# A two-layer graph network on one core: node degrees from a second load of the adjacency, leftover filter coefficients in 32x32 tiles, and a norm placed later

## The chip, the cores and the metric

One core of a Trainium2 chip, everything in float32. The metric is device microseconds of one execution of the whole program; lower is better. The median of several runs is compared.

## What is computed

The input x holds 128 samples of 128 nodes with 256 features, adj one 128x128 matrix per sample. Two layers follow each other, each as a residual under a layer norm.

```python
# layer 0
in_degrees = jnp.sum(adj, axis=-1)
norm = jnp.power(in_degrees + 1e-06, -0.5)[..., None]
f_hom = jnp.einsum('bnd,de->bne', x, theta) * norm
f_hom = jnp.einsum('bnm,bmd->bnd', adj, f_hom) * norm
f_het = jnp.einsum('bnd,de->bne', x, W_h)
gate = jax.nn.sigmoid(jnp.einsum('bnd,de->bne', x, W_t) + b_t)
out = jax.nn.elu(gate * f_hom + (1.0 - gate) * f_het)
x = _layernorm(x + out)
# layer 1
xc = jnp.transpose(x, (0, 2, 1))
h = relu(bn(conv1d(xc, conv1_w)))              # kernel size 1
h = bn(conv1d(h, conv2_w, pad=8))              # 17 taps along the nodes
x_conv = jnp.transpose(relu(h + xc), (0, 2, 1))
# ... a second branch x_nmp: exp(-distance) of 3 coordinates times relu(x @ w_msg.T)
# ... a GRU cell of [x_conv, x_nmp] and x, then x = _layernorm(x + cell)
```

## The kernel before, in words

Samples go in pairs: pair p holds samples 2p and 2p+1, so there are 64 pairs. Nodes lie on the 128 partitions. The kernel runs in three stages.

**Layer-0 rounds** (`a_round`, from line 597). One round per pair, software-pipelined: round t projects pair t (`l0_project`: products f_ps at L371, gate_ps at L376), mixes it over the adjacency (`l0_mix`, mix_ps L397), finishes pair t-1 (`l0_gate`, `l0_elu`, `l0_norm`), turns and runs conv1 for pair t-3 (`l1_turn`, `l1_front`) and makes the transform of pair t-4 (`l1_analyse`, coef_ps L486). The order on all engines is the order in which the program is written (`tc.manual_schedule` over TensorE, SyncE, DVE, ScalarE and GpSimd), so an instruction that waits holds back what stands behind it on its engine. Eight PSUM banks are handed out in turn.

The degrees of a pair come from its own adjacency tile, which is loaded already transposed: `l0_degrees` transposes the two 128x128 blocks on TensorE (adj_ps, L351), sums them on DVE (L353) and raises the sums to -1/2 on GpSimd (`inv_sqrt`, L206 and L207). It stands at the end of a round for the next pair, and ScalarE multiplies the projection by the result as it evicts f_ps (hom, L380).

The 17-tap convolution along the nodes is done by a transform of length 136 = 128 + 8: `l1_analyse` makes 136 coefficients of every channel and sample from h, ScalarE writes them to the resident tile H (L490), which is laid out as (channel half, coefficient, sample).

The same transform of the filter taps is made inside these rounds, spread over them as extra work. `w_unit` (32 units, about every second round) makes the first 128 coefficients of 4 x 1 filter rows from a tap tile wt: four products of 17 rows by 128 columns in four row tiles of TensorE, 512 columns wide (w_ps, L502), evicted by ScalarE and stored to w_d. The last 8 coefficients, the leftovers, are made by `v_unit` in 19 sets of 7 filter rows: a block table TL of 7 copies of the small transform (built by 14 small DMAs of `leftover_table`) times a second load of the taps (vt, `v_load`), one product of 128x128 by 512 columns (wl_ps, L529), evicted by DVE (L533) and stored by `v_store`.

`l0_norm` of pair t-1 (DVE nb L327, two ScalarE activations L329) follows directly behind the projection of pair t.

**Tap stage** (loop at line 819). For each of 68 pairs of coefficients k, the taps w_d[k] are loaded and multiplied with H: the samples are the columns of the stationary operand. y_ps (L826) takes four products of 256 columns with `coefs(m, c)` as weights. For all but the first k there is a three-product complex form: GpSimd adds the two tap blocks (ws, L834), DVE adds two rows of H (hs, L836), z_ps (L839) multiplies them. In the trace a float32 matmul is two instructions, each with its own weight load.

**Layer-1 groups** (loop from line 1220): the way back of the transform, the second branch and the GRU cell for groups of four samples. The change leaves it alone.

All loads of the rounds and of the tap stage stand in SyncE's queue (SP) in program order; `in_blocks` (L140) loads x in blocks for DVE's 32x32 transpose `l0_turn` of the next pair; every second round `load_blocks` fetches two pairs into the one buffer xb. `w_load` (L170) fills the two buffers of wt.

Of the kernel before, what the change touches and what calls it, by code (L numbers as in the profile page):

```python
# [34 lines left out]
def gnn_layers_kernel(ctx: ExitStack, tc: tile.TileContext, a: dict, out: bass.AP):  # L35
# [49 lines left out]
    A, T = AT2[:, 0, :], AT2[:, 1, :]  # L85
    S = const.tile([P, P], F32, tag="S", name="S")
    SL = const.tile([P, P], F32, tag="SL", name="SL")
    FS = P // TAPS
    TL = taps.tile([P, P], F32, tag="TL", name="TL")
# [5 lines left out]
    vt = taps.tile([P, 2, D], F32, tag="vt", name="vt")  # L95
    wt = [taps.tile([P, 2, D], F32, tag=f"wt{i}", name=f"wt{i}") for i in range(NW)]


# [28 lines left out]
    def bank(name):  # L127
        return ps.tile([P, 512], F32, tag="ps", name=name)
# [75 lines left out]
    def inv_sqrt(dst, src, eps, width):  # L204

        nc.gpsimd.tensor_scalar(dst, src, eps, 1.0, ALU.add, ALU.mult)  # L206
        nc.gpsimd.tensor_tensor(dst, dst, neg_half[:, 0:width], ALU.pow)  # L207
# [79 lines left out]

    def way_back():

        nc.gpsimd.memset(TL, 0.0)  # L290

        nc.gpsimd.memset(vt[96:], 0.0)
# [15 lines left out]
    def leftover_table(i):  # L308

        cols = TL[:, 0 : ML * FS].rearrange("p (r i k) -> p r i k", r=2, i=FS)  # L310
        for r in range(2):
            nc.sync.dma_start(cols[i * TAPS : (i + 1) * TAPS, r, i, :], T[0:TAPS, P + r : M : 2])

    def norm_stats(src, n, name):

# [31 lines left out]
    def l0_degrees(p):  # L347
        s = st[p]
        adj = bank(f"adj_ps_{p}")
        for j in range(J):  # L350
            nc.tensor.transpose(adj[:, nodes(j)], s["adjT"][:, j, :], ident)  # L351
# [4 lines left out]
        inv_sqrt(norm, norm, DEG_EPS, J)  # L356


    def l0_project(p, between, beside):
# [121 lines left out]
    def l1_analyse(p):  # L481
        h = st[p]["h"]
        for j in range(J):
            pa = bank(f"coef_ps_{p}_{j}")
            for c in range(NC):
                nc.tensor.matmul(  # L486
                    pa[:, c * M : (c + 1) * M], lhsT=h[:, j, c * P : (c + 1) * P], rhs=A,
                    start=True, stop=True,
                )
            nc.scalar.activation(  # L490
                H[:, :, :, p * J + j], pa[:, 0 : NC * M].rearrange("p (c m) -> p c m", c=NC), AF.Copy
            )


# [15 lines left out]
        )  # L510


    NV = -(-P // FS)
    s_v = {}

    def v_set(v):

        return FS * v, min(FS, P - FS * v)

    def v_load(v):  # L520
        f, n = v_set(v)
        nc.sync.dma_start(
            vt[0 : n * TAPS],
            a["conv2_wT"].rearrange("(c f) t o -> (f t) c o", c=NC)[f * TAPS : (f + n) * TAPS],
        )

    def v_unit(v):
        pl = bank(f"wl_ps_{v}")
        nc.tensor.matmul(  # L529
            pl, lhsT=TL, rhs=vt.rearrange("p i (o c) -> p i c o", c=NC), start=True, stop=True  # L530
        )
        ol = s_v[v] = taps.tile([ML * FS, NC * D], F32, tag="wl", name=f"wl_o_{v}")
        nc.vector.tensor_copy(ol, pl[0 : ML * FS])  # L533

    def v_store(v):
        ol = s_v.pop(v)
        f, n = v_set(v)
        h = ML // 2
        for r in range(2):
            nc.sync.dma_start(  # L540
                w_d[P // 2 : M // 2, r, f : f + n].rearrange("k f c o -> f k (c o)"),
                ol[r * h * FS : r * h * FS + n * h],
            )


    m_in = []

# [35 lines left out]
    warm = bank("warm_ps")  # L583
    for _ in range(WARM):
        nc.tensor.matmul(warm[:, 0:P], lhsT=ones, rhs=ones, start=True, stop=True)
    units = {2 + 2 * u - 2 * u // NU: u for u in range(NU)}
    rest = [t for t in range(4 + FS, NP - 1) if t not in units]
    units_v = {rest[v * (len(rest) - 1) // (NV - 1)]: v for v in range(NV)}
    hstack = ExitStack()
    H = None  # L590
    E = mybir.EngineType

    SOON = 3
    norms, ways = batch_norms(), way_back()
    tables = table(AT2, (node, lag))

    def a_round(t):
        nonlocal H
        def on(q, work):
            if 0 <= q < NP:  # L600
                work(q)

        def between():
            on(t - 1, l0_gate)
            on(t - 3, l1_turn)
            on(t - 4, l1_analyse)

        def beside():
            if 0 <= t <= SOON:
                l0_turn(t + 1)  # L610
            on(t - 1, l0_elu)
            if 0 <= t < SOON:
                l0_degrees(t + 1)

        if t > 1 and t % 2 == 1 and t + 1 < NP:
            load_blocks(t + 1, 2)
        l0_project(t, between, beside) if t >= 0 else between()
        on(t - 1, l0_norm)
        if t == 0:
            load_blocks(2, 2)  # L620
        if t == -1:
            next(tables)
        if not 0 <= t <= SOON:
            on(t + 1, l0_turn)
        on(t - 3, l1_front)
        on(t - 2, x1_store)
        if t > 0:
            load_x(t)
        if t + 2 < NP:
            if 2 <= t + 2:  # L630
                load(t + 2)
            if 3 <= t < 3 + FS:
                leftover_table(t - 3)
            if t == FS:
                v_load(0)
# [5 lines left out]
        if t - 1 in units_v:  # L641
            v_store(units_v[t - 1])
            if units_v[t - 1] + 1 < NV:
                v_load(units_v[t - 1] + 1)
        if t + 2 < NP:
            on(t - 2, load_back)
        on(t - 3, x1T_store)
        if not 0 <= t < SOON:
            on(t + 1, l0_degrees)
        if t == -1:  # L650
            next(tables, None)
        if t == 0:
            nc.sync.dma_start(conv1_w[:, :, 0:D], a["conv1_wT"].rearrange("(p c) e -> p c e", c=NC))
            nc.sync.dma_start(conv1_w[:, :, D:], a["w_seT"].rearrange("(p c) e -> p c e", c=NC))
            next(norms)
        if t == 1:
            next(norms)
            next(ways)
        if t == NP // 2:
            nc.scalar.dma_start(w_msg, a["w_msgT"].rearrange("(p c) e -> p c e", c=NC))  # L660
            nc.scalar.dma_start(b_msg, a["L1_gnn_b_msg"].partition_broadcast(P))
        on(t, l0_mix)
        if t == 2:
            next(norms, None)
        if t in (4, 5):
            next(ways, None)
        if t == SOON:
            sctx.close()
            hpool = hstack.enter_context(tc.tile_pool(name="hpool", bufs=1))
            H = hpool.tile([P, NC, M, NB], F32, tag="H", name="H")  # L670
        if 0 <= t < 2:
            w_load(t)
        if t - 1 in units and units[t - 1] + NW < NU:
            w_load(units[t - 1] + NW)
        if t in units_v:
            v_unit(units_v[t])
        if t in units:
            if t + 1 < NP:
                w_unit(units[t])

    with tc.manual_schedule(engines={E.PE, E.SP, E.DVE, E.Activation, E.Pool}):
        for t in range(-1, NP):
            a_round(t)
        last = NP - 1
        l1_turn(last - 2)
        w_unit(units[last])
        l0_gate(last)
        l1_analyse(last - 3)
        l1_front(last - 2)
# [3 lines left out]
        l0_elu(last)  # L693
        early = [m_project(0, "gate")]
        m_load(2)
        w_store(units[last])
        m_load(3)
        early[0][0]()
        l0_norm(last)
# [31 lines left out]
    pb = cpool("psB", 6, bctx, space=PSUM)  # L731

    def coefs(m, c):
        return H[:, c, m, :]

    left = cw.tile([P, NB, KD], F32, tag="left", name="left")
    right = cw.tile([P, NB, KD], F32, tag="right", name="right")
# [80 lines left out]
    with tc.manual_schedule(engines={E.Activation, E.Pool}):  # L818
        for k in range(M // 2):
# [12 lines left out]
            else:  # L832
                ws = yb.tile([P, NC, D], F32, tag="ws", bufs=2, name=f"ws_{k}")
                nc.gpsimd.tensor_tensor(ws, w[:, 0], w[:, 1], ALU.add)  # L834
                hs = yb.tile([P, NC, NB], F32, tag="hs", bufs=2, name=f"hs_{k}")
                nc.vector.tensor_tensor(hs, H[:, :, 2 * k, :], H[:, :, 2 * k + 1, :], ALU.add)  # L836
                pz = pb.tile([P, 2, D], F32, tag="py", name=f"z_ps_{k}")
                for c in range(NC):
                    nc.tensor.matmul(  # L839
# [461 lines left out]
```

## Time and profile before

| what | value |
|---|---|
| time, median of 3 runs | 1948.97 us (1948.71 to 1949.96) |
| the profiled execution | 1949.05 us, span 1947.3 us |
| TensorE matmul busy | 1932.2 us (99%) |
| DVE busy | 1497.8 us (77%) |
| ScalarE busy | 744.5 us (38%) |
| GpSimd busy | 674.3 us (35%) |
| granted TensorE clock | 0.998 |
| DMA | 279.64 MB, mean 144 GB/s |

The span is the stretch from the first to the last instruction; the execution's time holds a little more around it. In the lines shown, PE is TensorE's matmul, PEld its weight load (which overlaps PE), ACT is ScalarE, POOL GpSimd, SP SyncE; a "q" behind a name is its sequencer, which issues DMAs. L826 is line 826 of the kernel. A group's line gives engine, operation, out<-in, partitions x elements, count, busy us, mean ns of one, and idle time before it. A timeline's line gives start and length in us of like instructions merged into one. A source's line gives the duration as min/median/max in ns, and the first and last start. Ends of matmuls are modelled and overlap the next one; starts are measured.

### The profile page before, as it was taken

The numbers are of one execution on the slowest core, as the hardware profiler recorded it, in microseconds if no ns is written. First come the engines' busy times: TensorE is split into PE (matmuls) and PEld (weight loads), VectorE is DVE, ScalarE is ACT, GpSimd is POOL, SyncE is SP. The second block draws the span as 40 slices with busy tenths as digits, with TensorE's granted clock in tenths as the row PEclk, the third lists the DMA queues.
The fourth block names the chain that finished last, engine by engine and source line by source line (L and its number), as shares of the span: only waits on it lengthen the run. The fifth ranks groups of instructions, "written<-read, shape, count | busy, mean of one in ns | idle before, by whom it ended". The sixth has DMA issues, their size and how long they took to land.

```text
span 1947.3 us, 26718 instructions
## 1 busy us (share of the span) xinstructions
PE 1932.2 (99%) x8533; PEld 1324.2 (68%) x8533; DVE 1497.8 (77%) x3024; ACT 744.5 (38%) x1497; POOL 674.3 (35%) x891
## 2 busy tenths in 40 slices
PE   9999999999999999999999999999999999999997
PEld 6666666666666888866666666666666666666664
DVE  8888888888888644477777777877777777777777
ACT  4666666666666311122322322222332232223222
POOL 2111111111111455544434434434443443443431
PEclk9999999999999999999999999999999999999999
DMA  6888777878776899952212221221221222121100
GB/s 175 229 231 234 225 230 221 240 225 231 222 226 202 292 341 331 314 174 83 83 53 74 72 72 60 78 66 56 82 83 49 75 75 72 60 77 39 44 28 22
DMA packets 333572, 279.64 MB, mean 144 GB/s; under 512 B 149647, under 2 KB 275833, under 8 KB 333433
## 3 DMA queue, kind: packets, MB, share of 16 engines
q1 hardware_dynamic: 326729, 272.42, 45.7%
q10 hardware_dynamic: 6704, 5.52, 0.9%
q8 instruction: 69, 1.13, 0.2%
q14 instruction: 70, 0.57, 0.1%
HBM read 173.00 MB, written 104.86 MB: 143 GB/s over the span
## 4 chain that ended last, share of the span: by engine, by line
PE 93%; DVE 3%; DMA 1%; ACT 1%; POOL 1%; issue 1%; SPq 0%; POOLq 0%; ACTq 0%; DVEq 0%
PE g_ps L1150 43%; PE f_ps L371 10%; PE y_ps L826 6%; PE conv_ps L465 5%; PE gate_ps L376 5%; PE msg_ps L1006 4%; PE conv_ps L945 3%; PE z_ps L839 3%; PE nmp_ps L1084 3%; PE coef_ps L486 3%; PE mix_ps L397 2%; PE w_ps L502 2%; PE conv_ps L952 1%; PE wl_ps L529 1%; PE adj_ps L351 1%; PE dist_ps L1064 1%
## 5 line engine op out<-in xcount | busy, mean ns | idle before, releaser
L329 ACT ACTIVATE y<-y,nb_b,rstd_b 128x256 f32<-128x256 f32 x128 | 70.0, 593 | 561.6 <-DVE nb_b L327 561.6
L371 PE MATMUL f_ps<-w,xT 128*128 128x512 f32 x512 | 243.9, 599 | 1.8 <-DMA w<-in_L_gnn_W_h 1.0
L1211 POOL TENSOR_TENSOR u<-u,p 128x512 f32<-128x512 f32 x63 | 80.0, 1270 | 244.2 <-DVE p L1191 244.2
L371 PEld LDWEIGHTS f_ps<-w,xT 128*128 128x128 f32 x512 | 89.9, 189 | 99.3 <-issue 66.3
L1150 PE MATMUL g_ps<-t_h,sh 128*128 128x384 f32 x384 | 156.8, 490 | 0.0
L1150 PE MATMUL g_ps<-t_c,sc 128*128 128x384 f32 x384 | 155.2, 486 | 0.0
L1150 PE MATMUL g_ps<-t_m,sm 128*128 128x384 f32 x384 | 155.2, 486 | 0.0
L206 POOL TENSOR_SCALAR rstd_a<-mv_a 128x2 f32<-128x2 f32 x64 | 12.4, 193 | 379.9 <-DVE mv_a L320 379.9
L376 PEld LDWEIGHTS gate_ps<-w,xT 128*128 128x128 f32 x512 | 97.3, 190 | 67.8 <-issue 54.1
L376 PE MATMUL gate_ps<-w,xT 128*128 128x256 f32 x512 | 131.4, 379 | 0.0
L826 PE MATMUL y_ps<-wb,H 128*128 128x256 f32 x544 | 128.3, 379 | 0.0
L834 POOL TENSOR_TENSOR ws<-wb 128x512 f32<-128x512 f32 x67 | 94.9, 1418 | 85.0 <-PE z_ps L839 54.0
L465 PE MATMUL conv_ps<-conv_w,x1T 128*128 128x259 f32 x512 | 122.6, 381 | 0.0
L826 PEld LDWEIGHTS y_ps<-wb,H 128*128 128x128 f32 x544 | 103.4, 190 | 14.0
L380 ACT ACTIVATE hom<-f_ps,norm 128x256 f32<-128x256 f32 x128 | 60.8, 475 | 125.2 <-PE f_ps L371 123.9
L1111 ACT ACTIVATE o<-o 128x1024 f32<-128x1024 f32 (+1 forms) x65 | 67.6, 1040 | 107.0 <-POOL o L1212 58.8
L1150 PEld LDWEIGHTS g_ps<-t_c,sc 128*128 128x128 f32 x384 | 73.0, 190 | 50.9
L1150 PEld LDWEIGHTS g_ps<-t_m,sm 128*128 128x128 f32 x384 | 73.0, 190 | 50.9 <-DVE sm L1100 0.2
L465 PEld LDWEIGHTS conv_ps<-conv_w,x1T 128*128 128x128 f32 x512 | 96.9, 190 | 14.6
L1150 PEld LDWEIGHTS g_ps<-t_h,sh 128*128 128x128 f32 x384 | 71.7, 190 | 48.7
L1150 PE MATMUL g_ps<-w_hhT_w,cx1T 128*128 128x384 f32 x256 | 104.6, 492 | 0.0
L1150 PE MATMUL g_ps<-w_ihT_w,xcT 128*128 128x384 f32 x256 | 103.0, 486 | 0.0
(247 smaller groups left out, 4430.4 us busy)
## 6 DMA issues: line engine op xcount, KB each, us to landing
wb<-w_d SPq DMA_DIRECT2D x68, 512.0 KB
w_d<-w_o SPq DMA_DIRECT2D x32, 1024.0 KB
y_d<-yb SPq DMA_DIRECT2D x68, 256.0 KB
x<-in_x SPq DMA_DIRECT2D x64, 256.0 KB
x_d<-x SPq DMA_DIRECT2D x64, 256.0 KB
cx1T<-x1T_d SPq DMA_DIRECT2D x64, 256.0 KB
yt<-y_d SPq DMA_DIRECT2D x32, 512.0 KB
cx<-x_d SPq DMA_DIRECT2D x32, 512.0 KB
```

Source lines behind the costliest of these rows:

```text
L329: nc.scalar.activation(dst[:, q, :], src[:, q, :], AF.Identity, bias=nb[:, q : q + 1], scale=rstd[:, q : q + 1],)
L371: nc.tensor.matmul(pf, lhsT=xT[:, c, nodes(j)], rhs=w0[:, c, 0 : 2 * D], start=(c == 0), stop=(c == NC - 1),)
L376: nc.tensor.matmul(pg[:, j * D : (j + 1) * D], lhsT=xT[:, c, nodes(j)], rhs=w0[:, c, 2 * D : 3 * D], start=(c == 0), stop=(c == NC - 1),)
L380: nc.scalar.activation(hom[:, j, :], pf[:, 0:D], AF.Copy, scale=norm[:, j : j + 1])
L465: nc.tensor.matmul(ph[:, 0 : D + CO], lhsT=s["x1T"][:, c, nodes(j)], rhs=conv1_w[:, c, :], start=(c == 0), stop=(c == NC - 1),)
L486: nc.tensor.matmul(pa[:, c * M : (c + 1) * M], lhsT=h[:, j, c * P : (c + 1) * P], rhs=A, start=True, stop=True,)
L826: nc.tensor.matmul(py[:, blk, :], lhsT=coefs(blk if k == 0 else 2 * k + 1 - blk, c), rhs=w[:, blk, c, :], start=(c == 0), stop=(c == NC - 1),)
L834: nc.gpsimd.tensor_tensor(ws, w[:, 0], w[:, 1], ALU.add)
L1006: nc.tensor.matmul(pm[:, pr * P : (pr + 1) * P], lhsT=s["fh"][i][:, pr, :], rhs=factors["g"][i], start=True, stop=True, skip_group_check=True,
L1111: nc.scalar.activation(rz, rz, AF.Tanh, scale=0.5)
L1150: nc.tensor.matmul(pg[:, lo : lo + 3 * P], lhsT=s[f"f{kind}"][i][:, pr, :], rhs=factors[kind][i], start=(k == 0), stop=(k == 2), skip_grou ...
L1211: nc.gpsimd.tensor_tensor(u4, u2, p5, add)
```

## The change

Four things are done.

Degrees: the first 16 pairs keep `l0_degrees`. For pairs 16 to 63 the adjacency is loaded a second time in three blocks of 32 samples, eight DMAs of 256 KB each, into the part of H that belongs to the last 32 samples and is not yet written: partitions are (quarter of the summed index, sample). GpSimd adds the 32 rows down to one, one product with a selection matrix per block (`degrees_make`) adds the four quarters and leaves 128 nodes x 32 samples, DVE adds the epsilon and GpSimd raises all 32 columns to -1/2 at once. The loads stand at the end of SP's part of rounds 4 to 11, and of every second round from 12 to 42; the sums follow a round later, at most two steps per round.

Layout of H: from (channel half, coefficient, sample) to (group of four coefficients, sample, coefficient within the group), so that the spare part consists of rows of 128 contiguous words. ScalarE's eviction, `coefs` and hs follow.

Leftovers: `v_unit`, TL, vt and `leftover_table` go. `v_set` makes the leftovers of two units from the same tap buffers wt that the two units have used: 16 products of 17 rows by 32 columns by 256, in 32x32 tiles, four row tiles times four column tiles, into four banks; ScalarE evicts them, four DMAs store them. There are 16 sets, each in the round behind every second unit; `w_load` of the next unit's taps then stands behind the set.

Order: from round 4 on `l0_norm` stands behind `l0_turn` and `l1_front`. The units' rounds shift slightly.

```diff
-    units = {2 + 2 * u - 2 * u // NU: u for u in range(NU)}
-    rest = [t for t in range(4 + FS, NP - 1) if t not in units]
-    units_v = {rest[v * (len(rest) - 1) // (NV - 1)]: v for v in range(NV)}
+    units = {2 + 2 * u - (u > 10) - (u > 20): u for u in range(NU)}
+    sets = {t + 1: u // 2 for t, u in units.items() if u % 2}
...
+    parts = {4 + i: (1, i) for i in range(2 * Q)}
+    parts.update({12 + 2 * i: (2 + i // (2 * Q), i % (2 * Q)) for i in range(4 * Q)})
+    made = {max(t for t in parts if parts[t][0] == w) + 4: w for w in range(1, NB // K)}
...
+    HI = 4
+    def spare(at, n):
+        return H[:, at : at + n, NB - K :, :].rearrange("p r b i -> p r (b i)")
+    def degrees_rows(w):
+        return spare((w - 1) % 2 * K, K)
+    def degrees_load(w, i):
+        q, n = i % Q, K // 2
+        at = slice(i // Q * n, i // Q * n + n)
+        v = adjT.rearrange("(q s) b n -> q b s n", q=Q)
+        nc.sync.dma_start(
+            degrees_rows(w)[q * K : (q + 1) * K, at, :], v[q, w * K : (w + 1) * K, at, :]
+        )
+    def degrees_add(w, i):
+        rows_ = degrees_rows(w)
+        def add(at, n):
+            nc.gpsimd.tensor_tensor(rows_[:, 0:n], rows_[:, 0:n], rows_[:, at : at + n], ALU.add)
+        if i % Q == Q - 1:
+            half = K // 2
+            for at in range(i // Q * half, (i // Q + 1) * half, HI):
+                if at:
+                    yield add(at, HI)
+        if i == 2 * Q - 1:
+            add(2, 2)
+            yield add(1, 1)
+    def degrees_make(w):
+        t = bank(f"deg_ps_{w}")
+        nc.tensor.matmul(
+            t[:, 0:K], lhsT=degrees_rows(w)[:, 0, :], rhs=sums["pick"], start=True, stop=True
+        )
+        norm = degrees_norm(w)
+        nc.vector.tensor_scalar(norm, t[:, 0:K], DEG_EPS, None, ALU.add)
+        nc.gpsimd.tensor_tensor(norm, norm, sums["root"], ALU.pow)
+        for p in range(w * K // J, (w + 1) * K // J):
+            st[p]["norm"] = norm[:, p * J % K : p * J % K + J]
...
             nc.scalar.activation(
-                H[:, :, :, p * J + j], pa[:, 0 : NC * M].rearrange("p (c m) -> p c m", c=NC), AF.Copy
+                H[:, :, p * J + j, :],
+                pa[:, 0 : NC * M].rearrange("p (r i) -> p r i", i=HI), AF.Copy,
             )
...
-    def v_unit(v):
-        pl = bank(f"wl_ps_{v}")
-        nc.tensor.matmul(
-            pl, lhsT=TL, rhs=vt.rearrange("p i (o c) -> p i c o", c=NC), start=True, stop=True
-        )
-        ol = s_v[v] = taps.tile([ML * FS, NC * D], F32, tag="wl", name=f"wl_o_{v}")
-        nc.vector.tensor_copy(ol, pl[0 : ML * FS])
+    def v_set(i):
+        po = [bank(f"wl_ps_{i}_{r}") for r in range(Q)]
+        for e in range(2):
+            t = wt[(2 * i + e) % NW].rearrange("p i (o c) -> p i c o", c=NC)
+            for c in range(NC):
+                g = slice(K * (NC * e + c), K * (NC * e + c + 1))
+                for r in range(Q):
+                    k = slice(K * r, K * r + TAPS)
+                    nc.tensor.matmul(
+                        po[r][g, 0:D], lhsT=T[k, M - K : M], rhs=t[k, c], start=True, stop=True
+                    )
+        ol = s_v[i] = taps.tile([P, Q, D], F32, tag="wl", name=f"wl_o_{i}")
+        for r in range(Q):
+            nc.scalar.activation(ol[:, r, :], po[r][:, 0:D], AF.Copy)
...
         l0_project(t, between, beside) if t >= 0 else between()
-        on(t - 1, l0_norm)
+        if t <= SOON:
+            on(t - 1, l0_norm)
...
             on(t + 1, l0_turn)
         on(t - 3, l1_front)
+        if t > SOON:
+            on(t - 1, l0_norm)
...
+        if t - 1 in sets:
+            v_store(sets[t - 1])
+            if 2 * sets[t - 1] + NW + 1 < NU:
+                w_load(2 * sets[t - 1] + NW + 1)
+        if t in parts:
+            degrees_load(*parts[t])
-        if not 0 <= t < SOON:
+        if not 0 <= t < SOON and t + 1 < K // J:
             on(t + 1, l0_degrees)
+        if t in made:
+            degrees_make(made[t])
...
         on(t, l0_mix)
+        if t - 1 in parts:
+            adds.append(degrees_add(*parts[t - 1]))
+        for _ in range(2):
+            while adds and next(adds[0], adds) is adds:
+                adds.pop(0)
...
-        if t - 1 in units and units[t - 1] + NW < NU:
-            w_load(units[t - 1] + NW)
-        if t in units_v:
-            v_unit(units_v[t])
+        if t in sets and t + 1 < NP:
+            v_set(sets[t])
+            w_load(2 * sets[t] + NW)
         if t in units:
-            if t + 1 < NP:
-                w_unit(units[t])
+            w_unit(units[t])
...
     def coefs(m, c):
-        return H[:, c, m, :]
+        return H[:, (c * M + m) // HI, :, m % HI]
```

More of the change, by code (lines that the diff above doesn't have):

```diff
@@ L87, in gnn_layers_kernel @@
     SL = const.tile([P, P], F32, tag="SL", name="SL")
-    FS = P // TAPS
-    TL = taps.tile([P, P], F32, tag="TL", name="TL")
     conv1_w = acon.tile([P, NC, D + CO], F32, tag="conv1_w", name="conv1_w")
@@ L94, in gnn_layers_kernel @@
     NW = 2
-    vt = taps.tile([P, 2, D], F32, tag="vt", name="vt")
     wt = [taps.tile([P, 2, D], F32, tag=f"wt{i}", name=f"wt{i}") for i in range(NW)]
@@ L288, in way_back @@
     def way_back():
-        nc.gpsimd.memset(TL, 0.0)
-        nc.gpsimd.memset(vt[96:], 0.0)
         back = small.tile([P, 1], F32, tag="back", name="back", bufs=1)
@@ L306, in way_back @@
         nc.vector.tensor_scalar(SL, tS[:, P : 2 * P], 2.0 / L, None, ALU.mult)
[L308 to L312, printed above, removed]
     def norm_stats(src, n, name):
@@ L356, in l0_degrees, with degrees_begin, degrees_norm @@
         inv_sqrt(norm, norm, DEG_EPS, J)
+    sums = {}
+    HI = 4
+    adds = []
+    def spare(at, n):
+        return H[:, at : at + n, NB - K :, :].rearrange("p r b i -> p r (b i)")
+    def degrees_begin():
+        n = 2 * K
+        sums["pick"], sums["root"] = (spare(n + i, 1)[:, 0, 0:K] for i in range(2))
+        nc.gpsimd.memset(sums["root"], -0.5)
+        nc.gpsimd.tensor_tensor(sums["pick"], ident[:, 0:K], ident[:, K : 2 * K], ALU.add)
+        for q in range(2, Q):
+            nc.gpsimd.tensor_tensor(sums["pick"], sums["pick"], ident[:, q * K : (q + 1) * K], ALU.add)
+    def degrees_rows(w):
+        return spare((w - 1) % 2 * K, K)
+    def degrees_norm(w):
+        return H[:, NC * M // HI - 1, NB - K :, w]
+    def degrees_load(w, i):
[27 more added lines that the diff above has]
+            st[p]["norm"] = norm[:, p * J % K : p * J % K + J]
     def l0_project(p, between, beside):
@@ L510, in w_store, with v_store @@
         )
-    NV = -(-P // FS)
     s_v = {}
[L516 to L524, printed above, removed]
-        )
-    def v_unit(v):
-        pl = bank(f"wl_ps_{v}")
-        nc.tensor.matmul(
-            pl, lhsT=TL, rhs=vt.rearrange("p i (o c) -> p i c o", c=NC), start=True, stop=True
-        )
-        ol = s_v[v] = taps.tile([ML * FS, NC * D], F32, tag="wl", name=f"wl_o_{v}")
-        nc.vector.tensor_copy(ol, pl[0 : ML * FS])
[L535 to L543, printed above, removed]
+    def v_set(i):
[12 more added lines that the diff above has]
+            nc.scalar.activation(ol[:, r, :], po[r][:, 0:D], AF.Copy)
+    def v_store(i):
+        ol = s_v.pop(i)
+        w = w_d.rearrange("k s (r u) c o -> u c (k s) r o", r=Q)
+        for e in range(2):
+            for c in range(NC):
+                lo = K * (NC * e + c) + K - ML
+                nc.sync.dma_start(w[2 * i + e, c, P:M], ol[lo : lo + ML])
     m_in = []
@@ L631, in a_round @@
                 load(t + 2)
[L632 to L635, printed above, removed]
         else:
@@ L640, in a_round @@
             w_store(units[t - 1])
[L641 to L644, printed above, removed]
         if t + 2 < NP:
@@ L669, in a_round @@
             hpool = hstack.enter_context(tc.tile_pool(name="hpool", bufs=1))
-            H = hpool.tile([P, NC, M, NB], F32, tag="H", name="H")
+            H = hpool.tile([P, NC * M // HI, NB, HI], F32, tag="H", name="H")
+            degrees_begin()
         if 0 <= t < 2:
             w_load(t)
-        if t - 1 in units and units[t - 1] + NW < NU:
-            w_load(units[t - 1] + NW)
-        if t in units_v:
-            v_unit(units_v[t])
+        if t in sets and t + 1 < NP:
+            v_set(sets[t])
+            w_load(2 * sets[t] + NW)
         if t in units:
-            if t + 1 < NP:
-                w_unit(units[t])
+            w_unit(units[t])
     with tc.manual_schedule(engines={E.PE, E.SP, E.DVE, E.Activation, E.Pool}):
@@ L685, in gnn_layers_kernel @@
         l1_turn(last - 2)
-        w_unit(units[last])
+        v_set(sets[last])
         l0_gate(last)
@@ L695, in gnn_layers_kernel @@
         m_load(2)
-        w_store(units[last])
+        v_store(sets[last])
         m_load(3)
@@ L835, in gnn_layers_kernel @@
                 hs = yb.tile([P, NC, NB], F32, tag="hs", bufs=2, name=f"hs_{k}")
-                nc.vector.tensor_tensor(hs, H[:, :, 2 * k, :], H[:, :, 2 * k + 1, :], ALU.add)
+                rows_k = slice(2 * k // HI, NC * M // HI, M // HI)
+                ha, hb = (H[:, rows_k, :, (2 * k + i) % HI] for i in range(2))
+                nc.vector.tensor_tensor(hs, ha, hb, ALU.add)
                 pz = pb.tile([P, 2, D], F32, tag="py", name=f"z_ps_{k}")
```

## The prediction

> **What bounds the kernel now.** I read the page first, then the windows by stage, then TensorE's timeline inside one round of each kind. The page's engine row and chain come first.
>
> ```profile
> PE 1932.2 (99%) x8533; PEld 1324.2 (68%) x8533; DVE 1497.8 (77%) x3024; ACT 744.5 (38%) x1497; POOL 674.3 (35%) x891
> PE 93%; DVE 3%; DMA 1%; ACT 1%; POOL 1%; issue 1%; SPq 0%; POOLq 0%; ACTq 0%; DVEq 0%
> ```
>
> TensorE is the bound over the whole span. The windows below hold the two stages that the change touches: 300 to 400 us lies in the layer-0 rounds (to about 648 us), 660 to 800 us in the tap stage. Columns: span, PE, PEld, DVE, ACT, POOL busy with counts, clock, DMA share, GB/s. The last line is what TensorE waited for between 20 and 640 us (total, times, longest).
>
> ```profile
> 300.00:400.00 100.00, 100.00 (x436) 66.78 (x435) 84.35 (x186) 66.93 (x154) 17.80 (x40) 1.00 0.81 235
> 660.00:800.00 140.00, 140.00 (x649) 123.00 (x648) 67.35 (x123) 21.92 (x58) 77.34 (x56) 1.00 0.95 325
> ```
>
> ```profile
> PE coef_ps L486 <- ACT h L473: 0.8, 1, 0.8
> PE f_ps L371 <- ACT coords L472: 0.7, 2, 0.5
> ```
>
> So a TensorE microsecond removed in either stage is worth one, and one added costs one; waits of other engines cost nothing until TensorE meets them. DVE (84 of 100 us) is next, and the change only lightens it there. Matmuls overlap, so I price an operation by the distance between starts. TensorE's timeline in a round with a leftover set, then in one with a tap unit, then in the tap stage:
>
> ```profile
> 292.86 0.38 PE L351 MATMUL adj_ps<-ident,adjT 128*128 128x128 f32 x2
> 293.07 1.03 PE L397 MATMUL mix_ps<-hom,adjT 128*128 128x256 f32 x4
> 293.94 1.06 PE L529 MATMUL wl_ps<-vt,TL 128*128 128x512 f32 x2
> 294.84 1.45 PE L371 MATMUL f_ps<-w,xT 128*128 128x512 f32 x3
> ...
> 302.89 1.03 PE L397 MATMUL mix_ps<-hom,adjT 128*128 128x256 f32 x4
> 303.85 1.18 PE L502 MATMUL w_ps<-wt,AT 17*128 17x512 f32 x8
> 304.96 1.98 PE L371 MATMUL f_ps<-w,xT 128*128 128x512 f32 x4
> ```
>
> ```profile
> 699.29 1.89 PE L826 MATMUL y_ps<-wb,H 128*128 128x256 f32 x8
> 701.02 1.03 PE L839 MATMUL z_ps<-ws,hs 128*128 128x256 f32 x4
> ```
>
> Two degree transposes take 0.21 us, a leftover set 0.90, a tap unit 1.11; eight y instructions take 1.73, so 216 ns each, with no gap to the next group.
>
> **Degrees.** Two transposes go from 48 of 64 pairs: 48 x 0.216 (0.108 each: 0.38 for two less 0.272 for one) = -10.4 us of TensorE. With them go 48 DVE reductions (408 ns, -20 us of DVE) and 48 GpSimd power steps (0.2 + 0.7 us, -43 us of POOL). Three new products of 32 columns, two passes each, cost at least one weight-load pace per pass: 3 x 2 x 0.108, +0.7 us; 0.2 more each would be +1.2. The 24 loads (256 KB each, 6.3 MB) take the place of 19 leftover loads (4.3 MB): DMA at 0.81 stays below full. GpSimd's sums per block of 32 samples are seven adds of 128x512 (1.27 us by its row L1211) and two small ones, 10 us, at most two per round in an engine that is 18% busy there. They stand behind a load issued a round earlier; what is queued behind them is the next pair's rstd, wanted half a round later, so I take nothing. The power over 32 columns is different: the rows give 699 ns for 2 columns and 1019 for 4.
>
> ```profile
> L207 POOL TENSOR_TENSOR norm<-norm,neg_half 128x2 f32<-128x2 f32 x64 | 44.7, 699 | 5.4
> L207 POOL TENSOR_TENSOR scale<-scale,neg_half 128x4 f32<-128x4 f32 x1 | 1.0, 1019 | 0.1
> ```
>
> That is 160 ns a column, so 0.7 + 30 x 0.16 = 5.5 us. The first block is made at the end of round 15 and round 16 wants it 1.9 us in (after its first f_ps): ScalarE would stand up to 4 us, and the mix near the round's end would be met about 1 us late. The other two blocks are made two rounds ahead. Once: +1 us (0 to 4).
>
> **Leftover taps.** Removed: 19 sets x 0.90 = -17.1 us. Added: 16 sets of 16 products, two passes of 256 columns each, in 32x32 tiles; the trace has tiles of 32 rows by 128 columns, but none of 32 columns. One 256-column pass over this interleaved operand is 0.90/4 = 0.226 us. The tap unit shows that four row tiles run together: eight instructions of 512 columns in 1.11 us, two passes of 0.452 plus 0.21, and the mix before it took 0.96 where it took 0.87 ahead of a set: 0.30 us of overhead for the change of shape. A set is then 0.30 + n x 0.226, with n the passes that follow one another. All 16 tiles together: n = 2, 0.75, with some issue time 0.85, 13.6 us in all. No overlap between column tiles of one row tile: n = 8, 2.1 us, 33.8 in all. No overlap at all: n = 32, 7.5 us, 120 in all. I take n = 5: within a row tile the products are queued as first pass, second pass, next product, and the second pass has to follow the first, so only each second pass overlaps the next first. 0.30 + 1.13 = 1.43, x 16 = +22.9 us. Evictions go from DVE (-13 us) to ScalarE: 64 x 0.38 (het's row) = +24 us, against which the coefficient eviction writes runs of four words instead of single ones (668 ns now for 272 elements, where het takes 379 for 256): about -30. ScalarE stays near 67%.
>
> The Trainium skill speaks to n: TensorE: Matmul & The Clock Gate (Part 3, packing) gives 10.6 times for 16 tiles of 32x32 and a span of one matmul plus about 4 ns per tile. That favours n = 2, for one-pass operands; by it, as an estimate, the sum below would be 9 us lower.
>
> **The coefficients' new layout.** H goes from contiguous samples to one word in every four, and all 544 weight loads of y read it so. This is the term that decides. The loads of the trace, min/median/max ns:
>
> ```profile
> L826 PEld LDWEIGHTS y_ps<-wb,H x544: 190/190/190, 648.1 to 823.1; 128*128 128x128 f32 x182
> L351 PEld LDWEIGHTS adj_ps<-ident,adjT x128: 137/139/152, 5.3 to 619.4; 128*128 128x128 f32 x128
> L451 PEld LDWEIGHTS x1T_ps<-ident,x x8: 194/201/209, 633.9 to 640.9; 128*128 128x128 f32 x8
> 640.71 0.63 PE L451 MATMUL x1T_ps<-ident,x 128*128 128x128 f32 x4
> ```
>
> y's load starts with the matmul ahead of it and ends 26 ns before the next (190 of 216). The two transposes differ in one thing: adjT is read word after word, x every second word, and that takes 62 ns more. Linear in the step, every fourth word takes 139 + 3 x 62 = 325. Four x1T matmuls run 116 ns apart ((0.63 - 0.28)/3) with loads of 201, so a matmul starts about 85 ns before its load's recorded end: 325 means a pace of 240. y then runs at 240 instead of 216: 544 x 24 = +13 us. Lower bound: if y's load grows by 62 only, 252 - 85 = 167 stays hidden, 0. Upper bound: if the next matmul waits for the recorded end, 544 x (325 - 216) = +59. I take 13, by x1T's row, the nearest. DVE's sum hs reads the same words, but DVE is half idle there.
>
> SBUF — State Buffer (the note on cachelines) says that each access to a new 16-byte line pays, and that two hits per line are needed to hide it; every fourth word has one. It speaks against this layout and agrees that the next doubling hurts; it gives no time.
>
> **Moves.** l0_norm goes behind the turn, conv1 and their evictions: DVE's nb waited 9.7 us in all for rstd, which TensorE never met, so no gain. x1 comes at most one turn and two evictions (1.4 us) later; it is stored in the next round and read back a round after, which covers it. Uncovered it would cost that 1.4 a round. w_load now stands in SP's queue at the end of a set's round and waits for the set's matmuls; queued behind it are the next round's loads. In five rounds (25, 29, 33, 37, 41) these are the 512 KB of blocks, issued today right behind the turn:
>
> ```profile
> 282.75 1.91 SPq L140 DMA_DIRECT2D xb<-in_x  x4
> 292.28 0.71 DVE L441 STREAM_TRANSPOSE xT<-xb 128x512 f32<-128x512 f32 x1
> ```
>
> They would start some 4 us later (round's end at 284.9 plus four issues of 0.4), leaving about 3.6 us to land before the turn; x1b's 256 KB are met 4 to 6 us after their issue. A late turn of up to 2 us has 2 us of room before the next round's f_ps. I take +1 us in all, bounds 0 and 8.
>
> **Sum.** -10.4 + 0.7 - 17.1 + 22.9 + 13 + 1 + 1 = +11.1 us. The profiled execution took 1949.05 us, span 1947.3 plus 1.75 around it, 0.08 above the median of 1948.97. 1949.05 + 11.1 = 1960.1; against the median 1960.0.
>
> **Rivals.** First, the other side: y's loads stay behind its matmuls. It decides as long as a load's pace stays under 216 ns, a record under about 300. Then the sum is -1.9 with n = 5 (1947), -11.2 with n = 2 (1938), and without the two waits -13.2 (1936). For it: 26 ns of idle plus the 85 of overlap; against it: the 62 ns of a single doubling. Chance 0.34: 0.26 for a time below 1945, 0.08 for one within 0.2% of the time before (about what a measurement of this kernel can tell from no change). Second, loads show but all 16 tiles run together: 11.1 - 9.3 = +1.8, 1951, chance 0.06. Third, the work doesn't leave the path as said: ScalarE's coefficient evictions and GpSimd's sums now share one tile, H, and if an eviction is made to wait for a sum's load, 24 loads x 4 us are +96 (2056); or the column tiles don't overlap (+97 over my n = 5), or the loads cost 59 rather than 13 (2006). Nothing in the trace shows any of these; together 0.14. The forecast, loads that show and sets of 1.4 to 2.1 us (1957 to 1972), has the remaining 0.46.
>
> **How the numbers follow.** Faster 0.26, same 0.08 + 0.06 = 0.14, slower 0.46 + 0.14 = 0.60. The range goes from 1938 (loads hidden, tiles together) to 1976 (n = 8, 33.8 instead of 22.9, and 4 us more of waits): it leaves out the third rival and a sliver below. The forecast's own range is 1957 to 1972.
>
> **What would show it.** Right: y's weight loads near 325 ns and y's starts near 240 apart; sets' start to the next f_ps near 1.4 us; rounds from the 17th pair on 0.2 us shorter; H's evictions near 400 ns. Wrong: y's starts still 216 apart (then the kernel is faster), sets under 1 us, or TensorE waiting in the layer-0 rounds for hom, xT or coef_ps by more than 2 us in all.

## The result: 0.5% slower

After: 1958.39 us, median of 6 runs (1955.97 to 1961.1); before, in the same series, 1948.89 (1948.47 to 1949.96). Ratio 1.0048, 95% interval [1.0035, 1.0061]. The profiled execution after took 1961.1 us, span 1959.3, so it lies 2.7 us above its median; the runs after scatter over 5 us where those before scatter over 1.5.

The page after, engine row and chain of waits:

```profile
PE 1930.6 (99%) x8917; PEld 1334.8 (68%) x8917; DVE 1480.0 (76%) x2960; ACT 731.8 (37%) x1561; POOL 694.1 (35%) x827
PE 84%; DVE 5%; DMA 4%; ACT 2%; SPq 2%; issue 1%; POOL 1%; DVEq 0%; ACTq 0%; POOLq 0%
```

TensorE's busy time fell by 1.6 us, the span grew by 12. The chain shows the difference: TensorE carries 84% of it, where it carried 93%; DVE, DMA and SyncE's queue have come in.

The first y instruction and the first of the layer-1 groups (msg_ps) divide the span into three stages. I read these starts from the trace: the rounds end at 651.3 us (before 648.4, +2.9), the tap stage lasts 185.3 (before 176.2, +9.1), the rest 1122.8 (before 1122.7). So the rounds, from which some 13 us of TensorE's work had gone, became longer, and the tap stage grew. The same two windows as before:

```profile
300.00:400.00 100.00, 93.83 (x455) 61.77 (x455) 75.92 (x168) 58.70 (x153) 18.18 (x24) 1.00 0.83 230
660.00:800.00 140.00, 140.00 (x618) 134.66 (x618) 70.36 (x118) 20.75 (x55) 85.09 (x55) 1.00 0.92 308
```

In the rounds TensorE stands for 6 of 100 us, at a DMA share of 0.83. In the tap stage it stands nowhere, and does 618 instructions where it did 649. What TensorE waited for between 20 and 640 us:

```profile
PE f_ps L416 <- DVE xT L486: 8.3, 9, 1.4
PE conv_ps L510 <- DVE x1T L486: 3.9, 3, 1.8
PE f_ps L416 <- ACT w_o L551: 1.0, 1, 1.0
PE f_ps L416 <- PE wl_ps L570: 0.7, 2, 0.4
PE coef_ps L531 <- ACT h L518: 0.5, 1, 0.5
```

The turns on DVE are late, and DVE in turn waits for the blocks that they turn (100 to 640 us; the second list is the kernel before, where this was next to nothing):

```profile
DVE x1T L486 <- DMA x1b<-x_d: 32.7, 18, 3.8
DVE xT L486 <- DMA xb<-in_x: 18.0, 15, 2.9
```

```profile
DVE x1T L441 <- DMA x1b<-x_d: 1.7, 2, 1.3
```

One such wait can be followed. SyncE's queue in round 30 and the start of round 31, then TensorE in round 31 (start, length, engine, line; a bracket gives the idle time before it and what ended it):

```profile
301.00 1.36 SPq L583 DMA_DIRECT2D w_d<-wl_o  x2
302.45 1.80 SPq L167 DMA_DIRECT2D wt<-in_conv_wT  x4
304.35 0.39 SPq L521 DMA_DIRECT2D x_d<-x  x1
...
306.86 3.33 SPq L137 DMA_DIRECT2D x1b<-x_d  x4
310.23 0.57 SPq L524 DMA_DIRECT2D x1T_d<-x1T  x1
310.84 0.43 SPq L373 DMA_DIRECT2D H<-in_adjT  x1
311.37 2.23 SPq L137 DMA_DIRECT2D xb<-in_x  x4
```

```profile
313.57 1.99 PE L510 MATMUL conv_ps<-conv_w,x1T 128*128 128x259 f32 x8 [1.81 <-DVE x1T L486]
...
317.98 1.95 PE L416 MATMUL f_ps<-w,xT 128*128 128x512 f32 x4 [0.44 <-DVE xT L486]
```

The stores of the set and its tap load stand ahead of the store of x1 (x_d); x1's blocks (x1b) can only be read once that store has landed, 2.5 us after its issue here; conv1 then stands 1.81 us for the turn. The second load of adj stands ahead of the next blocks (xb), and f_ps stands 0.44 us for those.

The terms that the prediction named, in the profile after: y's weight loads, a set with its neighbours, and the power over 32 columns.

```profile
L874 PEld LDWEIGHTS y_ps<-wb,H x544: 308/329/329, 651.0 to 835.0; 128*128 128x128 f32 x182
```

```profile
325.89 1.02 PE L442 MATMUL mix_ps<-hom,adjT 128*128 128x256 f32 x4
326.85 0.74 PE L570 MATMUL wl_ps<-wt,AT 17*32 17x256 f32 x32
327.51 1.98 PE L416 MATMUL f_ps<-w,xT 128*128 128x512 f32 x4
329.33 1.03 PE L421 MATMUL gate_ps<-w,xT 128*128 128x256 f32 x4
...
331.12 1.88 PE L416 MATMUL f_ps<-w,xT 128*128 128x512 f32 x4
332.84 1.03 PE L421 MATMUL gate_ps<-w,xT 128*128 128x256 f32 x4
```

```profile
L399 POOL TENSOR_TENSOR H<-H x3: 5471/5473/5475, 158.5 to 471.2; 128x32 f32<-128x32 f32 x3
```

A weight load of y took 326 ns in the mean (before 190) and y's starts lie 233 apart (before 216). A set takes 0.66 us from its start to the next f_ps. The change of shape costs time on both sides as well: the mix in front of the set lasts 0.96 us to the set's start (0.87 ahead of an old set, 293.07 to 293.94), and f_ps behind it 1.82 us to gate_ps, where the next one takes 1.72. The power takes 5.47 us.

### The profile page after: what moved, and what is told of

The parts are those of the page before. It is cut to its first block, busy times and chain, and to the rows that moved or that the text cites. A ratio compares the mean times of both kernels' runs of the same rounds, so it can differ in the third digit from the quotient of the medians.

```text
span 1959.3 us, 27365 instructions
## 1 busy us (share of the span) xinstructions
PE 1930.6 (99%) x8917; PEld 1334.8 (68%) x8917; DVE 1480.0 (76%) x2960; ACT 731.8 (37%) x1561; POOL 694.1 (35%) x827
## 4 chain that ended last, share of the span: by engine, by line
PE 84%; DVE 5%; DMA 4%; ACT 2%; SPq 2%; issue 1%; POOL 1%; DVEq 0%; ACTq 0%; POOLq 0%
PE g_ps L1200 43%; PE f_ps L416 7%; PE y_ps L874 6%; PE msg_ps L1056 4%; PE conv_ps L510 4%; PE gate_ps L421 3%; PE z_ps L889 3%; PE conv_ps L995 3%; PE nmp_ps L1134 3%; DMA xb<-in_x 2%; PE coef_ps L531 2%; SPq L137 2%; PE mix_ps L442 2%; PE w_ps L548 1%; DMA w_d<-w_o 1%
## 5 line engine op out<-in xcount | busy, mean ns | idle before, releaser
L874 PE MATMUL y_ps<-wb,H 128*128 128x256 f32 x544 | 137.7, 397 | 0.0
L882 POOL TENSOR_TENSOR ws<-wb 128x512 f32<-128x512 f32 x67 | 106.8, 1596 | 82.1 <-PE z_ps L889 62.1
L874 PEld LDWEIGHTS y_ps<-wb,H 128*128 128x128 f32 x544 | 132.0, 326 | 1.7
L886 DVE TENSOR_TENSOR hs<-H 128x256 f32<-128x256 f32 x67 | 48.2, 720 | 82.9 <-PE z_ps L889 82.2
```

Source lines behind the costliest of these rows:

```text
L874: nc.tensor.matmul(py[:, blk, :], lhsT=coefs(blk if k == 0 else 2 * k + 1 - blk, c), rhs=w[:, blk, c, :], start=(c == 0), stop=(c == NC - 1),)
```

## The experiments

All were run in 5 rounds against the kernel before, whose median in these series was 1948.7 to 1949.2 us. "Rounds" and "tap stage" are the two stretches from the traces (before: 648.4 and 176.2 us).

**e1, the layout alone.** The kernel before with H in groups of four (ScalarE's eviction, coefs and hs follow), nothing else.

```diff
+    HI = 4
...
-            H = hpool.tile([P, NC, M, NB], F32, tag="H", name="H")
+            H = hpool.tile([P, NC * M // HI, NB, HI], F32, tag="H", name="H")
...
-        return H[:, c, m, :]
+        return H[:, (c * M + m) // HI, :, m % HI]
...
```

> The kernel before with one part of the change: H laid out in groups of four coefficients (the eviction, coefs and hs follow), nothing else. If the strided weight load alone makes the tap stage longer, y's loads take 326 ns and its starts lie 233 apart as in the changed kernel, 544 x 17 = +9.3 us, 1958 us, and TensorE waits in the rounds for as little as before (under 2 us). Rival: the layout also disturbs the rounds (ScalarE's eviction in runs of four words, DVE's hs): then more than +9.3, with TensorE waiting for coef_ps or hom.

Measured: 1958.51 us, 1.0048 [1.0034, 1.0061], +9.8 us. Rounds 647.7, tap stage 185.8. The layout costs what the whole change costs, all of it in the tap stage; so everything else in the change adds up to about nothing.

**e2, the sets alone.** The kernel before with v_set, its stores, the new rounds of the units and the new place of w_load.

> The kernel before with the leftovers in 32x32 tiles from the units' own tap buffers, with their stores, the units' new rounds and the later w_load; degrees, layout of H and place of l0_norm as before. TensorE's work: 16 sets of 0.67 us for 19 of 0.90, -6.5 us. If the waits of the changed kernel come from SyncE's queue (four stores of 0.7 us a set, tap loads that wait for the set, block loads behind them), a part shows here: 3 to 8 us of waits for xT and x1T, 1945 to 1951 us. If they come from l0_norm's place or from the second load of adj, none shows: 1942.5 us.

Measured: 1951.47 us, 1.0014 [1.0005, 1.0023], +2.7 us. The sets take 13.4 us in the rounds with their waits, where the 19 old ones took 17.2; the change of shape around them adds 0.2 us each, 3.2 in all. Without waits TensorE's work falls by about 3 us, not by the expected 6.5, and the rounds last 651.5. Neither xT nor x1T, whose lateness was expected, is in TensorE's list. It has another first line:

```profile
PE f_ps L416 <- ACT coords L517: 4.7, 6, 1.2
```

ScalarE, which now evicts the sets, frees banks late; that the evictions are what makes it late was not tried.

**e3, the norm put back.** The changed kernel with l0_norm directly behind the projection in all rounds, as before.

```diff
-        if t <= SOON:
-            on(t - 1, l0_norm)
+        on(t - 1, l0_norm)
...
-        if t > SOON:
-            on(t - 1, l0_norm)
```

> The changed kernel with l0_norm back in its old place, directly behind the projection. If the late norm is what makes the loads late (x1 is ready some 3 us later, SyncE waits for the store of x1 to land before it issues what is read back, and all loads queue behind that), most of the 16 us of waits go: 1943 to 1947 us. If SyncE's queue is too full for other reasons, the time stays within 4 us of the changed kernel's: 1954 to 1960 us.

Measured: 1969.01 us, 1.0101 [1.0087, 1.0115]: 10.6 us slower than with the late norm. So the move, which I had priced at nothing and then suspected, gains. DVE's waits, 100 to 640 us, then TensorE's, show how:

```profile
DVE nb_a L315 <- POOL rstd_a L204: 21.0, 38, 0.9
```

```profile
PE f_ps L416 <- DVE xT L486: 12.5, 12, 2.2
```

With the norm early, nb stands in front of the turn in DVE's queue and waits 21.0 us in 38 rounds for GpSimd's rstd (9.7 in the kernel before); in the changed kernel this line is not in the list. A turn that comes late anyway then comes later. That the 10.6 us come about in this way is read from the waits; it was not tried by itself.

**e4, H in groups of two.** The changed kernel with pairs of coefficients side by side instead of four; the spare part then has rows of 64 words, and the sums halve them five times.

```diff
-    HI = 4
+    HI = 2
...
```

> The changed kernel with H in groups of two coefficients instead of four, so that y's weight loads read every second word. The second load of adj goes into rows of 64 words (half of the nodes per DMA, still 24 DMAs of 256 KB), and GpSimd's sums are five halving adds per half. If the load's duration follows the step, it is near 250 ns, stays behind the 216 ns of its neighbour's matmul, and the tap stage is back at 176 us: -9.3 us against the changed kernel, 1949 us. Rival: any interleaving of the weights costs the matmul: starts stay near 225 to 233 and the time at 1954 to 1958 us.

Measured: 1950.0 us, 1.0004 [0.9995, 1.0012], 8.4 us below the changed kernel. Tap stage 177.1.

```profile
L868 PEld LDWEIGHTS y_ps<-wb,H x544: 195/196/197, 647.7 to 823.5; 128*128 128x128 f32 x182
```

Every second word costs 6 ns a load and is hidden; every fourth costs 136. The step lies between the two.

**e5, the tap load later.** The changed kernel with one load (four issues) moved.

```diff
             v_set(sets[t])
-            w_load(2 * sets[t] + NW)
...
         if t > 0:
             load_x(t)
+        if t - 1 in sets:
+            w_load(2 * sets[t - 1] + NW)
```

> The changed kernel with one move: the tap load that waits for a set's matmuls leaves the end of the set's round and goes into the next round, behind the block loads, the store of x1 and the load of x. If that wait at the head of SyncE's queue is what makes blocks and x1 late, 4 to 8 us of the 16 us of waits go: 1950 to 1954 us. If SyncE's queue is late because of the number of its issues, nothing changes: 1956 to 1960 us.

Measured: 1953.62 us, 1.0024 [1.0015, 1.0033], 4.8 us below the changed kernel, tap stage unchanged at 185.3. TensorE's waits for xT fell from 8.3 to 2.5 us, those for x1T from 3.9 to 0.8. (The profiled run after is the slowest of its 6, that of e5 the fastest of its 11, so these lists differ by more than the medians do.) So the place of this load in SyncE's queue costs 4.8 us. Whether by its wait for the set or by its four issues ahead of the blocks is not separated, and the wait alone is not enough. SyncE's waits in this load, 20 to 640 us, in the changed kernel and in e7 (below):

```profile
SPq L167 <- PE wl_ps L570: 7.3, 9, 1.2
```

```profile
SPq L167 <- PE wl_ps L570: 28.7, 14, 3.3
```

In e7 it waits four times as long, and TensorE's list there adds up to 2.9 us.

**e6, the stores of the sets on ScalarE's queue.**

```diff
-                nc.sync.dma_start(w[2 * i + e, c, P:M], ol[lo : lo + ML])
+                nc.scalar.dma_start(w[2 * i + e, c, P:M], ol[lo : lo + ML])
```

> The changed kernel with one move: the four stores of a set are issued by ScalarE's queue instead of SyncE's (64 issues of about 0.68 us, 44 us off SyncE in the rounds). If SyncE's issue time is what makes the loads late, 6 to 12 us go: 1946 to 1952 us. If it is the waits in its queue or the bytes, nothing: 1956 to 1960 us. ScalarE is 65% busy there; should its lateness count, hom and coef_ps appear among TensorE's waits.

Measured: 1962.24 us, 1.0065 [1.0052, 1.0077], 3.9 us slower than the changed kernel. This was no clean trial of the issue time: the stores left SyncE's queue, but waits for them entered it. The two lines of SyncE's waits that the changed kernel does not have:

```profile
SPq L167 <- DMA w_d<-wl_o: 32.2, 13, 4.1
SPq L137 <- DMA w_d<-wl_o: 10.6, 2, 5.8
```

**e7, no second load.** The changed kernel without the second load of adj, the sums and degrees_make; all pairs are transposed on TensorE.

```diff
-        if t in parts:
-            degrees_load(*parts[t])
-        if not 0 <= t < SOON and t + 1 < K // J:
+        if not 0 <= t < SOON:
             on(t + 1, l0_degrees)
-        if t in made:
-            degrees_make(made[t])
...
```

> The changed kernel without its second load of adj, GpSimd's sums and degrees_make: all pairs take degrees from TensorE's transposes; sets, layout and late norm stay. TensorE's work grows by 48 x 0.216 = 10.4 us. If the 24 loads cause most of the waits, these fall from 16 to about 4 us and the time is 1955 to 1958 us; if the sets' loads and stores alone cause them, 1966 to 1970 us.

Measured: 1955.82 us, 1.0037 [1.0024, 1.0049]: 2.6 us faster than the changed kernel, with 10.4 us more on TensorE. The new way of the degrees costs some 13 us of waits to save 10.4. TensorE's list shrinks to two lines:

```profile
PE conv_ps L510 <- DVE x1T L486: 1.5, 3, 0.8
PE coef_ps L531 <- DVE hom L447: 1.4, 1, 1.4
```

**e8, three moves at once.** Groups of two, stores on ScalarE's queue and the tap load later, put together before e6 was known.

> The changed kernel with H in groups of two, the stores of sets on ScalarE's queue, and the tap load of the set behind the next round's block loads. TensorE's own work is 15.6 us below the kernel before. If SyncE's queue is the cause of the waits, they fall from 12 to about 4 us: 1937 to 1941 us. If not, 1947 to 1950 us.

Measured: 1957.68 us, 1.0047 [1.0033, 1.0061], 7.7 above e4. A miss, and the same one as e6: SyncE waits 22.2 us in the tap load and 12.2 in the blocks for the stores of the sets.

**e9, groups of two and the tap load later**: e4 and e5 together.

> H in groups of two and the tap load of a set behind the next round's block loads; the stores of sets stay on SyncE's queue. If the two gains are independent, the rounds are those of e5 (642 us to the first y) and the tap stage that of e4 (177 us): 1942 to 1946 us, the first version that beats the kernel before. If the waits only change their place in the queue, as in e8, 1948 to 1952 us.

Measured: 1947.51 us, 0.9992 [0.9983, 1.0000], 2.5 below e4. Tap stage 176.7, rounds of the profiled run 643.4. The profiled run was the fastest of 11 (1944.51 to 1951.89); the median lies 1.5 us above the expected interval.

**e10, the stores and the second tap load one round further back** as well, behind the next round's block loads.

```diff
         if t - 1 in sets:
             w_load(2 * sets[t - 1] + NW)
+        if t - 2 in sets:
+            v_store(sets[t - 2])
+            if 2 * sets[t - 2] + NW + 1 < NU:
+                w_load(2 * sets[t - 2] + NW + 1)
...
-        if t - 1 in sets:
-            v_store(sets[t - 1])
-            if 2 * sets[t - 1] + NW + 1 < NU:
-                w_load(2 * sets[t - 1] + NW + 1)
```

> As e9, and the stores of a set and its second tap load, eight issues of some 4.6 us together, go one round further back, behind the next round's block loads, store of x1 and load of x. If the number of issues ahead of the block loads is what is left of the waits (6 us in e5), 3 to 5 us of it go: 1938 to 1943 us. If the turnaround of x1 through memory or the pow is what is left, the time is that of e9 within 2 us.

Measured: 1950.44 us, 1.0006 [0.9997, 1.0015], 2.9 above e9. The expected gain did not come, and the time is not that of e9 either. So the number of issues ahead of the blocks is not shown to be what was left. The move has a price of its own, which could hide a gain of that size, a tap load that now comes too late itself:

```profile
PE w_ps L542 <- DMA wt<-in_conv_wT: 1.9, 2, 1.4
```

**e11, as e10 without the second load, the sums and degrees_make.**

> As e10 without the second load of adj, GpSimd's sums and degrees_make: TensorE's own work grows by 48 x 0.216 = 10.4 us. If the second loads cost waits only because the queue was crowded by the sets, they are nearly free in e10, and this kernel is 7 to 10 us slower than e10: 1946 to 1951 us. If they cost their 12 us in any order, this kernel is as fast as e10 or up to 3 us faster.

Measured: 1947.4 us, 0.9989 [0.9980, 0.9998], 3.0 below e10 with 10.4 us more on TensorE: again some 13 us of waits. It is level with e9 (1947.51), 1.8 us below the kernel before, and its 11 runs lie within 3 us (1945.73 to 1948.48).

**e12, as e11 with the 24 loads back.** They are issued and nobody reads them; the sums, the power and degrees_make are left out, and the degrees come from the transposes.

> As e11 with the 24 second loads back and nothing else of the new degrees: they are issued where e10 issues them, nobody reads them, GpSimd's sums, the pow over 32 columns and degrees_make stay out, and all pairs take degrees from TensorE's transposes. If the loads themselves make the waits (24 issues on SyncE and some 18,000 more packets on DMA engines that are busy for three quarters of the rounds), TensorE waits 8 to 12 us longer than in e11: 1955 to 1960 us. If GpSimd's sums and the pow make them, the time is that of e11: 1946 to 1949 us.

Measured: 1952.15 us, 1.0016 [1.0006, 1.0025], 4.75 above e11. It falls between the two theories: the loads alone make some 5 us of the 13. With the sums, the power and degrees_make in place of the transposes (e10), TensorE has 10.4 us less to do and the kernel is only 1.7 faster; the other 8 or 9 us come with these. DMA queues of e11 and e12, 100 to 640 us (packets, MB, share of 16 engines):

```profile
q1 hardware_dynamic: 185695, 117.75, 76.1%
```

```profile
q1 hardware_dynamic: 204417, 121.88, 80.4%
```

The loads add 4 MB and 19,000 packets, ten per cent, to engines that are busy for three quarters of the time. Whether their 5 us come from these packets or from the 24 issues on SyncE was not separated.

What GpSimd does beside it can be seen in the changed kernel. DVE beside two sums of 128x512, GpSimd at the same time, and DVE beside the power (158.52 to 163.99 us):

```profile
138.61 0.69 DVE L456 SCALAR_TENSOR_TENSOR hom<-gate,hom 128x512 f32<-128x512 f32 x1
139.34 1.64 DVE L457 SCALAR_TENSOR_TENSOR het<-hom,het 128x512 f32<-128x512 f32 x1
141.02 1.38 DVE L458 TENSOR_SCALAR gate<-het 128x512 f32<-128x512 f32 x1
```

```profile
138.82 3.29 POOL L381 TENSOR_TENSOR H<-H 128x512 f32<-128x512 f32 x2
```

```profile
159.31 0.69 DVE L456 SCALAR_TENSOR_TENSOR hom<-gate,hom 128x512 f32<-128x512 f32 x1
160.04 0.69 DVE L457 SCALAR_TENSOR_TENSOR het<-hom,het 128x512 f32<-128x512 f32 x1
```

het takes 1.64 us instead of 0.69 and the next instruction 1.38 instead of 0.43; each ends 0.3 to 0.6 us after a sum does (140.43 and 142.11). By the trace, 66 DVE instructions of the changed kernel's rounds overlap a sum, and they are 12.1 us longer together than the medians of their kinds; the 19 beside the power lose nothing, and in e12, which has no sums, none is longer than usual. So the sums, which I had let run beside DVE for nothing, hold it, though not every instruction: 20 of the 66 are more than 0.1 us longer (nb of L315, hom of L456, het and gate), while the turns, h and hom of L447, one of whose inputs lies in PSUM, run beside a sum at their usual length. Some 7 of the 12 us lie in the rounds of the first block (85 to 155 us, before the first power). There the distances between TensorE's starts hold 0.9 to 2.7 us of waits in the profiled runs of the changed kernel, e4, e5, e9 and e10 (2.7), and none in those of e7, e11 and e12, of which the last has the same loads. So a part of the 8 or 9 us does come from the sums. How much of the rest is theirs, beside the power and the lost slack, was not tried.

The Trainium skill has this in SBUF — State Buffer (Who interferes with whom; Terms): a DVE instruction with two SBUF inputs contends with a GpSimd instruction that reads SBUF, and the loser is fully blocked. The sums agree for hom of L456 and het; gate (L458), which has one input and is held too, is not covered by this sentence. The power does not agree: the two DVE instructions shown have two inputs and ran beside it at their usual 0.69 us.

## Why the prediction was right, and by which steps

The time was 1958.39 us against 1960.0, inside both ranges, and on the forecast's side. But apart from the layout the hit was luck: the sets were priced 9 us too high and the waits 14 us too low.

**What bounds it.** Right for the tap stage. In the rounds "a TensorE microsecond removed is worth one" failed: TensorE's own work there fell by 13.2 us (-10.4 + 0.7 for degrees_make, as predicted, - 17.2 + 13.7 for the sets with the change of shape around them), and the rounds got 2.9 longer. (The 15.6 us that e8's expectation counts leave the change of shape out.) The chain's 84% says it at a glance.

**Layout, +13.** The deciding term, and the right one: e1 gives +9.8, the starts 544 x 17 ns = +9.3. A load took 326 ns for the 325 predicted; the pace was 233 and not 240, since a matmul starts some 93 ns before its load's recorded end rather than 85. The 325 were luck all the same. "Linear in the step" is refuted by e4: every second word adds 6 ns to y's load, not 62. The prediction's own list hinted at it: y's load of contiguous words took 190 ns there and x1T's of every second word 201; only against adjT's 139, a load of the same size for which no run gives a reason, is the difference 62. The rule of the 16-byte line that the prediction quoted (SBUF — State Buffer, the note on cachelines: two hits a line hide the access) fits both: 196 ns with two words in a line, 326 with one.

**Sets, +22.9.** Too high by 9 us. A set takes 0.66 us, and the change of shape adds 0.09 to the mix in front and 0.10 to f_ps behind: 0.86 us, 13.7 in all without waits. That is the prediction's price for n = 2, which it did not take: 0.75 with the mix in front, 0.85 with "some issue time", 13.6 in all. So n is 2, and the reason that I gave for n = 5, that a second pass must follow its first, does not hold across the 16 tiles. By the Trainium skill's TensorE: Matmul & The Clock Gate (Part 3, packing), which the prediction weighed and set aside, the sum for the sets would have been 9 us nearer. The condition of the second rival held; its time did not, because of the next term.

**Waits, +2.** The largest wrong term. The distances between TensorE's starts in the rounds hold 17.7 us beyond the usual ones of their kinds (the medians over the profiled runs) in the profiled run after, where the kernel before has 1.5. These 16 us more and the 13.2 us less of work make the 3 us by which the rounds grew. What the prediction said of the waits:
- "They would start some 4 us later ... a late turn of up to 2 us has 2 us of room": right place, wrong size. w_load ahead of the next round's blocks costs 4.8 us (e5), not 1; that its wait is the reason was not separated from its issues.
- "DMA at 0.81 stays below full": that the engines are not full did not keep the second loads free. They cost about 5 us (e12 against e11).
- "What is queued behind them is the next pair's rstd, wanted half a round later, so I take nothing" looked at GpSimd's queue alone. The sums hold some of DVE's instructions (12.1 us in all), and with the power and degrees_make they cost 8 or 9 us (e10 against e12).
- The power: 5.5 us predicted, 5.47 measured; ScalarE stood 4.1 us for it once, and TensorE 1.2 about that time. The size came as predicted, the way not: the mix was met 0.3 us late, and the 1.2 us came at the next pair's f_ps, for a turn that DVE made late.

**Moves.** "l0_norm ... so no gain": wrong by 10.6 us in the changed kernel (e3). Its cover was priced; what a shorter wait in front of the turn is worth once the turns are late was not.

**The rivals.** "Loads hidden" fell with y's starts at 233. Of the third, column tiles that do not overlap fell with sets of 0.66 us, and loads that cost 59 us with e1's 9.8; the wait of ScalarE's evictions for the loads into H does not show. Two of the three marks that I set for wrong were hit although the time was right: sets under 1 us (0.66), and more than 2 us of waits for hom, xT or coef_ps (xT's 8.3). Of the marks for right, the weight loads (326 ns) and H's evictions (399 ns in the median) came; the sets near 1.4 us did not, y's starts came at 233 instead of 240, and the rounds grew.

**The account.** Singly: layout +9.8 (e1), sets +2.7 (e2), second load with its sums +2.6 (e7), late norm -10.6 (e3), together +4.5 for a measured 9.5. They do not add: e1 and e2 put a part into the kernel before, e3 and e7 take one out of the changed kernel, and the late norm may be worth more where turns are late (not tried in the kernel before). Without the second load (e7, +6.7) layout and sets leave -5.8 for it; this difference was not tried by itself.

## What to carry to other kernels

When work is taken off the bound engine, price again what stood hidden behind it: here queue positions, turnarounds through memory and an engine held by another, which cost almost nothing while TensorE was always busy, cost as much as was saved. A load that must wait for computation is better placed behind the loads that others wait for than ahead of them in their queue (4.8 us here for one moved line). Work in another shape also costs its neighbours: 0.2 us around each set here, a third of the set itself. And a layout chosen for a small side use (three blocks of sums) must be paid at its most frequent reader (544 weight loads).

## What the runs showed of the hardware that I had not expected

- Sixteen 32x32 tiles of float32, 32 instructions of 256 columns, take 0.66 us; the change of shape adds another 0.1 us on each side.
- A weight load of 128x128 float32 takes 190 ns from contiguous words, 196 from every second, 326 from every fourth.
- A GpSimd sum of 128x512 holds some DVE instructions until it ends (het with two inputs 0.69 to 1.64 us, gate with one 0.43 to 1.38), while turns run beside it unharmed; the power over 32 columns, four times as long, held none of the 19 beside it.
